# Statistics of a layer norm moved two steps earlier and behind the softmax division, and the root they feed put ahead of the masks on another engine

## The chip, the cores and the metric

The kernel runs on one core of a Trainium2 chip. The metric is the time of one execution on the device in microseconds (us). Two executions of one kernel usually differ by 0.1%, and all that are compared here are in the fast state. The engines are TensorE (PE, matmuls; PEld is its weight load), VectorE (DVE), ScalarE (ACT), GpSimd (POOL) and the queue that issues transfers (SP).

## The reference, cut to what matters

A block over x of shape (2, 256, 128, 128), all in float32: attention over time, attention over the 128 bands (a key counts if it is at most 16 bands away), and a feed-forward part. Each adds to x, and each has its own layer norm.

```python
xt = _ln(x, ...).transpose(0, 2, 1, 3)
x = x + _mha(xt, ..., H_T, causal).transpose(0, 2, 1, 3)
x = x + _mha(_ln(x, ...), ..., H_F, band)      # 16 bands to each side
h = gelu(_ln(x, ...) @ w1.T + b1)
x = x + (h @ w2.T + b2)
```

## The kernel before

Work is cut into groups of 512 tokens. 128 groups of attention over time come first. Then come 16 runs, each of 8 groups of attention over the bands (0 to 7 below) and the feed-forward of the same tokens (8 to 15). One turn of the loop ("step n") works on several groups at once. The order of the calls below is the order of each engine's queue, and in the traces DVE and POOL execute their parts in that order (PE's record has an exception, shown further down).

```python
def statistics(self):                      # DVE
    for i in range(NT): vector.bn_stats(stats[:, i, :], self.src()[:, i, :])
    for i in range(NT): vector.bn_aggr(self.mv[:, i, :], stats[:, i, :])

def root(self):                            # POOL
    gpsimd.tensor_scalar(self.rstd, self.mv[:, :, 1], EPS, None, ALU.add)
    gpsimd.tensor_tensor(self.rstd, self.rstd, path.k.mhalf, ALU.pow)

def normalize(self):                       # DVE, "xh": needs mv and rstd
    for i in range(NT):
        vector.tensor_scalar(self.xh[:, i, :], self.src()[:, i, :],
            self.mv[:, i, 0:1], self.rstd[:, i:i + 1], ALU.subtract, ALU.mult)
# turn: z = block transpose of xh (DVE), four DMAs z -> turned (DRAM)
# fetch: one DMA turned -> xnT, which the group's first matmuls read

# bands: first_mask = 6 affine_selects on POOL (two for each of 3 heads),
#        second_mask = one multiply by the band on DVE (the fourth head)
# divide, bands: t = rp*r0, u = op*r0, oT = (t - 2)*u   (DVE; rp and op in PSUM)
# divide, feed-forward: res = zp + res
# bias: 128x512 sums on POOL, in feed-forward steps only
```

The loop of the kernel before, cut. The groups of matmuls on PE are qp, kp, vp (projections), sp (scores), rp (row sums of the masked exponentials), op (weighted values), yp (output projection), and hp and zp (the two products of the feed-forward part).

```python
for n in range(-11, len(groups) + 2):
    ...
    do(n, "first_half", "first_function", "first_mask")   # sp or hp on PE; exp; masks
    ...
    do_at(n + 1, FeedForward, "fetch")
    do_at(n + 2, FeedForward, "normalize", "turn")
    do_at(n + 3, Attention, "normalize", "turn")
    do_at(n + 3, FeedForward, "statistics", "root")
    do_at(n + 4, OverTime, "root")
    if bands[2]: do(n, "second_mask")
    do(n - 1, "weigh")                                    # rp, op (bands); zp (feed-forward)
    do(n - 1, "invert_exactly" if turn else "invert")
    if bands[2] or turn: do(n - 2, "output", "finish")    # yp
    do(n - 1, "divide")
    if not turn: do(n, "second_half", "second_function")
    if not bands[2]:                                      # biases, the bands' statistics
        do(n, "second_mask", "bias"); do_at(n + A, OverBands, "bias"); ...
    do(n + 1, "queries_keys", ...)                        # qp, kp
    ...
```

## Time and profile before

| | before |
|---|---|
| median of the time | 2792.8 us |
| PE, DVE, ACT, POOL busy | 98%, 82%, 65%, 74% |
| undisturbed band step | 6.436 us |
| undisturbed feed-forward step | 7.006 us |

PE is the bound, and what can be won is its stall. Steps are timed from the first matmul of a group to the first of the next; the prediction says why.

The view below is the timeline of DVE and POOL about steps 5 and 6 of one run. Its columns are start, length, engine, line, operation, out<-in, shapes, count, and in brackets the idle time before it with what ended that.

```profile
1400.45 0.23 POOL L848 TENSOR_SCALAR rstd<-mv 128x4 f32<-128x4 f32 x1
1400.53 0.69 DVE L848 SCALAR_TENSOR_TENSOR oT<-t,u 128x512 f32<-128x512 f32 x1
1400.76 1.36 POOL L848 TENSOR_TENSOR rstd<-rstd,mhalf 128x4 f32<-128x4 f32 x1
1402.15 1.94 DVE L848 TENSOR_SCALAR xh<-x,mv,rstd 128x128 f32<-128x128 f32 x4 [0.94 <-POOL rstd L848]
1402.67 4.27 POOL L848 TENSOR_SCALAR_AFFINE_SELECT pf<-pf 128x512 f32<-128x512 f32 x6 [0.55 <-ACT pf L848]
```

POOL does the root of group 8 after the masks of step 5, so that root ends only at 1402.12. DVE is free at 1401.22 and waits 0.94 us for it. By then the masks of step 6 are about to start, and xh, next to them, takes 1.94 us in place of 1.11.

### The profile page before, as it was taken

What the parts mean: (1) busy time and instruction counts of PE and PEld (TensorE: products, weight loads), DVE (VectorE), ACT (ScalarE), POOL (GpSimd) and SP (SyncE); (2) the same over time, 40 slices, a digit from 0 to 9 for tenths busy, and PEclk for the clock granted to TensorE, in tenths of its full rate; (3) what the DMA queues carried; (4) which work ended last, traced back from release to release, by engine and by line L of the source; (5) the groups of instructions that cost most, each with busy time, mean ns of one, the idle gap of its engine ahead of it and who ended that gap; (6) DMA issues with size and microseconds to landing.
All of it is one profiled execution on the core that took longest, in us unless ns stands there. A gap on an engine that the chain in (4) does not pass through costs nothing.

```text
span 2791.8 us, 103916 instructions
## 1 busy us (share of the span) xinstructions
PE 2733.2 (98%) x42534; PEld 1844.4 (66%) x42534; DVE 2302.8 (82%) x6446; ACT 1800.7 (65%) x3328; POOL 2062.7 (74%) x2569
## 2 busy tenths in 40 slices
PE   4999999999999989999999999999999999999998
PEld 3666666666666656676776766767766667667666
DVE  5888888888888899788787797797887887977975
ACT  2888888788888866646546556456466475564563
POOL 3899999999999996666676676676666766766762
PEclk9999999999999999999999999999999999999999
DMA  5555555545555554543544534535435345444333
GB/s 119 134 148 136 139 139 142 145 131 151 133 142 142 140 137 111 131 123 99 140 102 112 132 104 123 129 96 130 127 100 136 104 108 130 103 125 115 83 99 85
DMA packets 471301, 343.70 MB, mean 123 GB/s; under 512 B 43296, under 2 KB 405152, under 8 KB 470816
## 3 DMA queue, kind: packets, MB, share of 16 engines
q1 hardware_dynamic: 469568, 335.92, 46.5%
q8 instruction: 337, 5.52, 0.8%
q14 instruction: 148, 1.21, 0.1%
q10 hardware_dynamic: 1248, 1.05, 0.1%
HBM read 169.03 MB, written 167.77 MB: 121 GB/s over the span
## 4 chain that ended last, share of the span: by engine, by line
PE 89%; DVE 4%; DMA 3%; POOL 3%; SPq 1%; issue 1%; ACT 0%; DVEq 0%; POOLq 0%
PE zp L848 16%; PE hp L848 15%; PE sp L848 12%; PE op L848 9%; PE qp L848 8%; PE rp L848 7%; PE vp L848 7%; PE kp L848 7%; PE yp L848 7%; DMA xnT<-turned 1%; DVE xh L848 1%; POOL pf L848 1%; DMA turned<-z 1%; POOL rstd L848 1%; POOL pt L848 1%
## 5 line engine op out<-in xcount | busy, mean ns | idle before, releaser
L848 POOL TENSOR_SCALAR_AFFINE_SELECT pf<-pf 128x512 f32<-128x512 f32 x768 | 520.9, 694 | 270.6 <-ACT pf L848 244.3
L848 ACT ACTIVATE hT<-hp,b 128x512 f32<-128x512 f32 x512 | 349.3, 687 | 548.6 <-PE hp L848 539.1
L848 DVE TENSOR_SCALAR xh<-x,mv,rstd 128x128 f32<-128x128 f32 x1536 | 624.0, 467 | 17.4 <-POOL rstd L848 17.4
L848 PEld LDWEIGHTS zp<-w2T_sb,hT 128*128 128x128 f32 x4096 | 476.3, 192 | 56.2 <-issue 54.0
L848 PE MATMUL zp<-w2T_sb,hT 128*128 128x128 f32 x4096 | 479.8, 275 | 0.1
L848 PE MATMUL hp<-xnT,w1f 128*128 128x512 f32 x1024 | 470.5, 596 | 6.7 <-DMA xnT<-turned 5.5
L848 POOL TENSOR_TENSOR rstd<-rstd,mhalf 128x4 f32<-128x4 f32 x384 | 446.9, 1164 | 32.0
L848 ACT ACTIVATE pt<-sp 128x384 f32<-128x384 f32 x1024 | 419.5, 497 | 58.8 <-PE sp L848 58.5
L848 PE MATMUL sp<-qT,kT 32*128 32x128 f32 (+1 forms) x8192 | 397.0, 316 | 0.9 <-ACT kT L848 0.8
L848 POOL TENSOR_SCALAR_AFFINE_SELECT pt<-pt 128x512 f32<-128x512 f32 x512 | 323.0, 652 | 79.6 <-ACT pt L848 79.6
L848 PEld LDWEIGHTS sp<-qT,kT 32*128 32x128 f32 x8192 | 315.3, 185 | 83.1 <-issue 31.4
L848 DVE BATCH_NORM_STATS2 stats<-x 128x6 f32<-128x128 f32 x1536 | 326.5, 273 | 7.7 <-DMA x<-in_x 7.7
L848 POOL TENSOR_SCALAR rstd<-mv 128x4 f32<-128x4 f32 x384 | 88.6, 231 | 298.7 <-DVE mv L848 297.5
L848 ACT ACTIVATE pf<-sp 128x512 f32<-128x512 f32 x512 | 264.3, 603 | 62.4 <-PE sp L848 59.1
L848 PEld LDWEIGHTS hp<-xnT,w1f 128*128 128x128 f32 x1024 | 181.1, 190 | 184.6 <-issue 107.9
L848 PE MATMUL qp<-xnT,wf 128*32 128x512 f32 (+1 forms) x1856 | 270.6, 600 | 26.1 <-DMA xnT<-turned 26.1
L848 PEld LDWEIGHTS yp<-wn,oT 128*32 128x32 f32 (+1 forms) x7808 | 234.1, 111 | 83.8 <-issue 61.8
L848 DVE STREAM_TRANSPOSE z<-xh 128x512 f32<-128x512 f32 x384 | 273.2, 712 | 18.8 <-DMA turned<-z 5.7
L848 PEld LDWEIGHTS vp<-wf,xnT 128*32 128x32 f32 (+1 forms) x7424 | 237.3, 113 | 75.0 <-issue 65.5
L848 PE MATMUL vp<-wf,xnT 128*32 128x128 f32 (+1 forms) x7424 | 271.9, 273 | 0.5 <-DVE t L848 0.5
L848 PE MATMUL yp<-wn,oT 128*32 128x128 f32 (+1 forms) x7808 | 271.1, 273 | 0.3 <-DVE t L848 0.3
L848 DVE TENSOR_TENSOR pf<-pf,band 128x512 f32<-128x512 f32 x128 | 117.4, 917 | 184.8 <-ACT pf L848 177.3
(90 smaller groups left out, 3974.0 us busy)
## 6 DMA issues: line engine op xcount, KB each, us to landing
turned<-z SPq DMA_DIRECT2D x1536, 64.0 KB, 2.1
xnT<-turned SPq DMA_DIRECT2D x384, 256.0 KB, 2.7
x<-in_x SPq DMA_DIRECT2D x128, 256.0 KB, 4.6
x<-res SPq DMA_DIRECT2D x256, 128.0 KB, 3.6
x<-x SPq DMA_DIRECT2D x128, 256.0 KB, 4.1
out<-res SPq DMA_DIRECT2D x256, 128.0 KB, 2.6
w1T_sb<-in_w1T ACTq DMA_DIRECT2D x1, 256.0 KB, 3.7
w2T_sb<-in_w2T ACTq DMA_DIRECT2D x1, 256.0 KB, 4.1
```

The lines of the kernel that those rows point to most:

```text
L848: return self.tc.keep_in_program_order(emit(*args, **kwargs))
```

## The change

Its intent: in band steps DVE should reach the division before it does statistics, and the root should be ready long before normalize needs it.

```diff
             do_at(n + 4, OverTime, "statistics")
             if bands[2] and feeds[1]:
                 self.scalar.preload_act_table_set(EXP_SET)
+            do_at(n + 4, FeedForward, "root")
             do(n, "first_half", "first_function", "first_mask")
@@
             do_at(n + 3, Attention, "normalize", "turn")
-            do_at(n + 3, FeedForward, "statistics", "root")
             do_at(n + 4, OverTime, "root")
@@
             do(n - 1, "divide")
+            do_at(n + 5, FeedForward, "statistics")
             if not turn:
                 do(n, "second_half", "second_function")
```

## The prediction

> **What bounds the kernel now.** I began with the page's busy shares and its list of groups, then read the chain of waits, then the timeline of one run of groups, engine by engine.
>
> ```profile
> PE 2733.2 (98%) x42534; PEld 1844.4 (66%) x42534; DVE 2302.8 (82%) x6446; ACT 1800.7 (65%) x3328; POOL 2062.7 (74%) x2569
> ```
>
> TensorE (PE) is busy for 98% of the span, so nothing that leaves its work alone can win 2%: its whole idle time is 2791.8 - 2733.2 = 58.6 us, and the first groups' load and the tail hold over half of that. Some stall also hides inside "busy", because a group of matmuls is drawn longer when one of them waits. To see it I took, from the trace, the time from the first matmul of each group to the first of the next, and subtracted the shortest such time of that kind.
>
> The change touches only the second half of the kernel (from 1046 us): 16 runs of 8 band-attention groups (0 to 7) followed by 8 feed-forward groups (8 to 15). "Step k" is the turn of the loop whose current group is k. An undisturbed band step costs PE 6.43 us, a feed-forward step 3.44 (hp) + 3.57 (zp) = 7.01 us. The excess over these, summed over the 16 runs, sits in few places:
>
> - Step 7, from scores (sp) to row sums (rp): 0.48 us in every run, 7.7 us in all.
> - Steps 8 and 9, before the first hp matmul: 3.3 us and 1.9 us, in 8 and 5 of the runs, up to 1.0 us each.
> - Step 15, before its first hp matmul: 4.0 us, in 9 runs, 1.7 us in the worst.
> - Step 9 before zp, 0.1 us a run, 1.5 us in all, whose cause I don't see.
>
> Together 18.4 us. That is the prize. The next lines, from timelines of single engines, say what each waits for.
>
> ```profile
> 1404.76 0.83 DVE L848 BATCH_NORM_STATS2 stats<-x 128x6 f32<-128x128 f32 x4
> 1405.51 0.36 DVE L848 BATCH_NORM_AGGREGATE mv<-stats 128x2 f32<-128x6 f32 x4
> 1405.79 0.66 DVE L848 TENSOR_TENSOR pf<-pf,band 128x512 f32<-128x512 f32 x1
> 1406.36 0.68 DVE L848 TENSOR_TENSOR x<-yp,x 128x512 f32<-128x512 f32 x1
> 1406.96 0.68 DVE L848 TENSOR_TENSOR t<-rp,r 128x512 f32<-128x512 f32 x1
> ...
> 1407.70 0.96 PEld L848 LDWEIGHTS sp<-qT,kT 32*128 32x128 f32 x26 [0.19 <-DVE t L848]
> ```
>
> In step 6 VectorE (DVE) does the statistics of a feed-forward group before the division (t, u, oT). Its t ends at 1407.64, and PE's scores of step 7, begun at 1407.20, go on at 1407.70: they need the bank that t reads.
>
> ```profile
> 1737.24 1.06 PE L848 MATMUL yp<-wn,oT 128*32 128x128 f32 x32
> 1739.23 3.67 PE L848 MATMUL hp<-xnT,w1f 128*128 128x512 f32 x8 [0.93 <-DMA xnT<-turned]
> ...
> 2114.26 1.88 PE L848 MATMUL hp<-xnT,w1f 128*128 128x512 f32 x4
> 2117.62 1.96 PE L848 MATMUL hp<-xnT,w1f 128*128 128x512 f32 x4 [1.48 <-DMA xnT<-turned]
> ```
>
> Steps 8 and 15 wait for the transposed input, whose transfers start when normalize and transpose (xh, z) end on DVE. These are late because xh is slow next to POOL:
>
> ```profile
> 2102.18 2.25 DVE L848 TENSOR_SCALAR xh<-x,mv,rstd 128x128 f32<-128x128 f32 x4
> 2105.10 3.11 DVE L848 TENSOR_SCALAR xh<-x,mv,rstd 128x128 f32<-128x128 f32 x4
> ...
> 2105.12 1.27 POOL L848 TENSOR_TENSOR res<-x,rows_sb 128x512 f32<-128x512 f32 x1
> 2106.34 1.27 POOL L848 TENSOR_TENSOR x<-x,orow 128x512 f32<-128x512 f32 x1
> ```
>
> Four xh take 1.11 us when POOL is idle or computes a root, 1.93 beside the masks, 2.95 to 3.1 beside the bias sums. So DVE is busy 6.97 us of the 7.00 from 2086 to 2093: nearly a second bound.
>
> **What the Trainium skill says.** "SBUF — State Buffer", section "Who interferes with whom": DVE and GpSimd share one port pair, whoever issues first keeps it for the instruction; a `tensor_scalar` in a 2-port mode contends, and so does a DVE instruction with two SBUF inputs against a GpSimd one that reads SBUF. The trace agrees: a single xh takes 0.34 us beside a root but 0.72 to 0.78 beside a mask; a mask takes 0.97 instead of 0.63 when DVE multiplies by the band; statistics, one SBUF input, keep 0.27 us whatever POOL does. "PSUM — Partial Sum Buffer", section "Engine vs sequencer instructions", calls the DVE and GpSimd queues strict FIFO: a root placed before the masks holds them back as long as it waits for mv. The trace shows such blocking where POOL sits 1.15 us idle for mv and the bias follows. "Perfetto Trace Analysis", section "GPSIMD Engine Instruction", warns that POOL durations are unreliable and start-to-start spacing is not; I use it below: six masks start to next start take 4.25 us.
>
> **The change part by part.** No instruction is added or removed. Each feed-forward group has 4 BN statistics and 4 aggregates, 1.15 us of DVE (1394.70 to 1395.85), and a root of 0.23 + 1.04 us on POOL, with the start about 0.09 after mv: 1.43 us from mv to the end. Statistics of group m move from step m-3, ahead of the division, to step m-5, behind it; the root goes to step m-4, ahead of the masks. So statistics leave steps 5 to 12 for 3 to 10.
>
> *Steps 3 and 4* gain 1.15 us of DVE. In step 4 DVE idled 1.18 us before its own mask for ACT (1391.30), so statistics at 1388.27 to 1389.42, xh to 1390.5 and z to 1391.2 just fit; step 5 has no normalize. Nothing moves on the path.
>
> *Step 6.* Before, xh(8) began at 1402.15 after 0.94 us of waiting for its root, took 1.94, and the statistics followed. Now its root is two steps old; DVE goes on straight from the statistics of group 10 (1402.3), with POOL in a root: xh ends 1403.4, z 1404.1 (was 1404.83), the band mask about 1405.1, t 1406.3 instead of 1407.64. The scores of step 7 then don't stall: 7.7 us won.
>
> *Steps 8 and 9.* z(8) is 0.77 earlier while PE arrives 0.48 earlier, so each wait shrinks by 0.29: of the eight waits (1.00, 0.53, 0.52, 0.38 and four at or under 0.27) about 1.3 of 3.3 us stays, 2.0 won. In step 7, xh(9) has no masks beside it and no statistics behind it; z(9) ends near 1410.4 instead of 1411.56, 0.67 more than PE's lead: 0.2 of 1.9 us stays, 1.7 won.
>
> *Steps 9 to 15.* A feed-forward step's order on POOL becomes root of the bands' statistics, root of the feed-forward, two biases, all behind statistics at the end of DVE's step, so that xh (right after these) lies beside roots. Groups of four at 1.6, 2.95, 2.95, 2.3 fall to about 1.1. At step 13 the first xh becomes fast, the second still meets biases; z(16) ends near 2107.6 instead of 2108.96. The fetch of group 15 stands behind that of group 16 in the queue, so its 1.5 us wait falls to about 0.2; the smaller ones go: 3.3 of 4.0 us won.
>
> Sum won: 7.7 + 2.0 + 1.7 + 3.3 = 14.7 us.
>
> *The cost: masks.* Before, step 5's masks ran 1396.23 to 1400.48, and PE wanted them at 1401.87, 1.4 us later. Now they wait for statistics and root: division ends 0.46 us after the scores start, statistics end at +1.53, root at +2.96, six masks with 4.25 at +7.21. They now also run under the division's last operation (two SBUF inputs), as under the band multiply: 0.34 more, +7.55, and some 0.08 for the semaphore. PE wants them one step and the scores later, at 6.43 + 1.10 = +7.53. That's a miss of about 0.1 us in steps 4 to 7; a miss at one step delays the next request, so it doesn't add up fully. I take 0.2 us a run, 3.2 us in all.
>
> Net: 14.7 - 3.2 = 11.5 us, 2792.8 to about 2781.3.
>
> **The rivals.** *POOL becomes the bound in steps 4 to 7.* For it: the slack of 1.4 us is spent to the last tenth. If each of four steps missed by 0.3 us, 19 us would be lost and the time be about 2797. Against: a late row sum shifts all that follows, which gives the masks of the next step as much. *DVE was no bound, and other waits take the stalls' place.* PE would start step 8 earlier and meet the transfer of xnT instead: only 5 us won, about 2788. For it: step 8 already waits in half of the runs; against it, z(8) comes earlier by more than PE does. *The relief in the feed-forward part is all there is*, because DVE has slack that PE can't use: 3 us, 2789. *Nothing new happens in masks*: 14.7 us, 2778.
>
> **Range and chances.** The centre is the net sum. The low end, 2775, is all 18.4 us won; the high end, 2790, is the second rival with masks on top. A change of 2% is 56 us: faster by it is beyond PE's stalls, slower by it would take 3.5 us in each of 16 runs, a pile-up of which I see no sign.
>
> **What would show it.** DVE busy falls by about 110 us a kernel: the xh groups lose 7 us a run (two of 0.82, then 0.5, 1.84, 1.84 and 1.2). Four xh of steps 6, 7 and 10 to 12 take 1.1 us. The statistics come right after oT in band steps, and DVE's wait for rstd, 17.4 us in the list of waits, is gone. The scores of step 7 take 1.17 in place of 1.65. Masks of steps 4 to 7 start 1.0 to 1.1 us later, and waits of PE for them appear, 0.1 us each. The prediction is wrong if the row sums stall by more than 0.3 us a step, if xh stays slow, or if hp waits for xnT as much as before.

## The result, and the profile after

The changed kernel took 2786.8 us (2784.58 to 2788.64, 4 runs) against 2792.91 us for the kernel before in the same rounds. The ratio is 0.9977, with a 95% interval of 0.996 to 0.9995. A second submission gave 2784.76 against 2793.06, ratio 0.9971 (0.996 to 0.9982). A ratio is the mean time of one kernel's fast runs over that of the other's in the same rounds, so it is not quite the ratio of the medians. The gain is 6 to 8 us. It lies inside the predicted range, at half to seven tenths of the 11.5 us that were predicted.

The page's first row after:

```profile
PE 2730.3 (98%) x42534; PEld 1867.5 (67%) x42534; DVE 2221.5 (80%) x6446; ACT 1800.0 (65%) x3328; POOL 2079.3 (75%) x2569
```

DVE lost 81 us of busy time: xh fell by 115 (624.0 to 509.2 us in the list of groups), and other operations, oT above all, got slower. PE lost only 3.

The next table gives mean step times over the 16 runs of groups, in the profiled executions. The steps not shown didn't change. "Floor" is the shortest of any run in the kernels here (the fourth row's 8.165 needs a wait just before it; 8.194 is what an undelayed run takes).

| us | floor | before | change | change again |
|---|---|---|---|---|
| scores of step 5 to step 6 | 6.435 | 6.436 | 6.460 | 6.457 |
| scores of step 6 to step 7 | 6.435 | 6.436 | 6.566 | 6.565 |
| scores of step 7 to first hp of step 8 | 3.845 | 4.532 | 4.181 | 4.035 |
| first hp of step 8 to first zp (step 9) | 8.165 | 8.292 | 8.388 | 8.402 |
| zp of step 14 to zp of step 15 (holds the first hp of step 15) | 7.006 | 7.261 | 7.021 | 7.007 |

The sum falls by 0.34 us a run in the first profile, 5.5 us in all (0.49 and 7.8 in the second). A further 1.3 us of that pair's difference in span (2791.8 to 2785.2) lies before the first band scores, where the change does nothing, so it is noise. The gains are at step 7 and step 15. In two rows, and for most runs in the fourth, the change made steps *longer*. The timeline of DVE and POOL in steps 5 and 6 shows how; the run is the one that the lines of before show.

```profile
1394.36 4.58 POOL L848 TENSOR_SCALAR_AFFINE_SELECT pf<-pf 128x512 f32<-128x512 f32 x6
...
1397.37 1.08 DVE L848 SCALAR_TENSOR_TENSOR oT<-t,u 128x512 f32<-128x512 f32 x1
...
1398.37 0.86 DVE L848 BATCH_NORM_STATS2 stats<-x 128x6 f32<-128x128 f32 x4
1399.15 0.36 DVE L848 BATCH_NORM_AGGREGATE mv<-stats 128x2 f32<-128x6 f32 x4
1399.43 1.08 DVE L848 TENSOR_SCALAR xh<-x,mv,rstd 128x128 f32<-128x128 f32 x4
1399.60 0.23 POOL L848 TENSOR_SCALAR rstd<-mv 128x4 f32<-128x4 f32 x1 [0.66 <-DVE mv L848]
1399.91 1.04 POOL L848 TENSOR_TENSOR rstd<-rstd,mhalf 128x4 f32<-128x4 f32 x1
...
1400.92 4.58 POOL L848 TENSOR_SCALAR_AFFINE_SELECT pf<-pf 128x512 f32<-128x512 f32 x6
```

Read it as a ring. The masks start at 1394.36. Their fifth select (affine_select, one of the six instructions of a mask group) ends at 1397.90 (single instructions of the trace). DVE's oT, issued at 1397.37, sits behind it and ends at 1398.45, 1.08 us long instead of 0.69. Statistics follow oT, the root follows them, and the next masks follow the root at 1400.92. The ring takes 6.56 us, and PE's step is 6.44. The Trainium skill's "SBUF — State Buffer", section "Who interferes with whom", says that a DVE instruction with two SBUF inputs contends with a GpSimd one that reads SBUF, for a port that is an exclusive lock. oT has two SBUF inputs, and it ends 0.54 us after the select, which agrees.

What PE sees of it, from its own timeline in the same step, is this:

```profile
1398.85 1.20 PE L848 MATMUL rp<-pf,ones 128*32 128x512 f32 x8
1399.74 1.08 PE L848 MATMUL op<-pf,v 128*32 128x128 f32 x30
1400.61 0.28 PE L848 MATMUL yp<-wn,oT 128*32 128x128 f32 x2
1400.64 0.28 PE L848 MATMUL op<-pf,v 128*32 128x128 f32 x2
...
1404.32 1.17 PE L848 MATMUL sp<-qT,kT 32*128 32x128 f32 x32
```

PE's wait for the masks shows in the first line. The rp group is drawn 1.20 us long, where every rp group of these steps before takes 1.07. In single instructions, the last select ends at 1398.94, and the third head's rp, which reads what that select wrote, starts at 1399.00, 0.14 us behind the first head's (0.01 before). In steps 5 to 7 of all 16 runs it starts 0.05 to 0.06 us after the end of that select, so it is the masks that it waits for. The rp groups of these steps are 0.02, 0.13 and 0.13 us longer than before, which is what the rows above grow by (the last of them shows in the third row's fastest run, 3.972 to a floor of 3.845). The list of waits leaves out gaps so short. Behind it the matmuls get out of order: two of the 32 op matmuls start after the first yp, though op comes first in the program. Each head has its own 32-column strip of the array, and the record fits one head's strip being late while the others go on (inferred; the trace doesn't name the strip). The scores of step 7 take 1.17 us where they took 1.65: the stall that the change was meant for is gone.

### The profile page after: what moved, and what is told of

It is laid out like the page before. It is cut to its first block, busy times and chain, and to the rows that moved or that the text cites. A ratio compares the mean times of both kernels' runs of the same rounds, so it can differ in the third digit from the quotient of the medians.

```text
span 2785.2 us, 103938 instructions
## 1 busy us (share of the span) xinstructions
PE 2730.3 (98%) x42534; PEld 1867.5 (67%) x42534; DVE 2221.5 (80%) x6446; ACT 1800.0 (65%) x3328; POOL 2079.3 (75%) x2569
## 4 chain that ended last, share of the span: by engine, by line
PE 93%; DVE 3%; DMA 2%; POOL 1%; issue 0%; SPq 0%; ACT 0%; DVEq 0%; POOLq 0%
PE zp L848 17%; PE hp L848 16%; PE sp L848 12%; PE op L848 10%; PE qp L848 8%; PE rp L848 8%; PE vp L848 8%; PE yp L848 7%; PE kp L848 7%; POOL pt L848 1%; DMA x<-in_x 1%; DVE xh L848 1%; DMA xnT<-turned 1%; DVE oT L848 0%; POOL rstd L848 0%; DVE stats L848 0%
## 5 line engine op out<-in xcount | busy, mean ns | idle before, releaser
L848 POOL TENSOR_SCALAR_AFFINE_SELECT pf<-pf 128x512 f32<-128x512 f32 x768 | 541.5, 720 | 173.5 <-ACT pf L848 147.1
L848 DVE TENSOR_SCALAR xh<-x,mv,rstd 128x128 f32<-128x128 f32 x1536 | 509.2, 392 | 0.4 <-POOL rstd L848 0.4
L848 POOL TENSOR_TENSOR rstd<-rstd,mhalf 128x4 f32<-128x4 f32 x384 | 441.3, 1149 | 32.0
L848 PE MATMUL sp<-qT,kT 32*128 32x128 f32 (+1 forms) x8192 | 389.5, 315 | 0.8 <-ACT kT L848 0.8
L848 PEld LDWEIGHTS yp<-wn,oT 128*32 128x32 f32 (+1 forms) x7808 | 240.8, 111 | 84.0 <-issue 63.2
L848 PE MATMUL yp<-wn,oT 128*32 128x128 f32 (+1 forms) x7808 | 277.9, 273 | 0.3 <-DVE t L848 0.3
L848 DVE TENSOR_TENSOR res<-zp,res 128x512 f32<-128x512 f32 x128 | 87.6, 685 | 234.8 <-PE zp L848 234.7
```

Source lines behind the costliest of these rows:

```text
L848: return self.tc.keep_in_program_order(emit(*args, **kwargs))
```

## The experiments

Theory A: after the change, masks, the division's last operation, statistics and root form a loop that is longer than PE's step (lock-step), and this eats half of the gain. Theory B: the masks cost nothing, and transfers into step 8 ate it. Theory C: only the feed-forward steps matter. Every kernel gave a correct result. The kernel before had medians of 2792.35 to 2793.06 us beside these runs.

| run | us | ratio to before (95%) |
|---|---|---|
| statistics alone | 2809.34 | 1.0061 (1.0047 to 1.0074) |
| root alone | 3008.8 | 1.0772 (1.0756 to 1.0788) |
| change in band steps alone | 2786.29 | 0.998 (0.9972 to 0.9988) |
| change in feed-forward steps alone | 2802.12 | 1.0032 (1.002 to 1.0044) |
| in the gap | 2776.26 | 0.9939 (0.9926 to 0.9953) |
| shorter root | 2785.68 | 0.9975 (0.9965 to 0.9986) |
| longer root | 2796.56 | 1.0013 (1.0006 to 1.0019) |
| one step earlier, nothing else | 2775.61 | 0.994 (0.9926 to 0.9954) |
| two groups in step 5 | 2783.64 | 0.9965 (0.9951 to 0.9978) |
| the change again | 2784.76 | 0.9971 (0.996 to 0.9982) |

Diffs are against the changed kernel unless they say otherwise.

**Statistics alone.** The statistics stay moved, and the root goes back behind the masks.

```diff
-            do_at(n + 4, FeedForward, "root")              # first
+            do_at(n + 3, FeedForward, "root")              # its old place
```

> The statistics moved as in the change, the root left where it was (step m-3, behind the masks). Theory A (lock-step of masks, division, statistics, root): the masks start at +1.9 us after the scores again, steps 5-6 and 6-7 fall from 6.46 and 6.57 to 6.44 us, the last operation of the division from 1.08 to 0.69 us; but the four xh of steps 6 and 7 lie beside masks again and take 1.9 us, so z(8) ends 4.1 us after the scores of step 6 as before and the first hp of step 8 waits about 0.5 us more a run for its transfer. Net about the changed kernel, 2783 to 2789. Theory B (the gain went to the transfer alone, masks cost nothing): no gain from free masks, later z, 2792 to 2796. Theory C (the gain is in the feed-forward steps, the band steps do not matter): as the changed kernel, 2786, with no shift inside.

This took 2809.34 us, slower than both kernels and outside all three ranges. The mask part came as theory A said: both band rows at 6.436 us. But the step from the first hp to zp took 9.16 us (8.39 with the change), and steps 11 and 12 (each from zp to zp) grew by 0.15 and 0.34. PE waits for transfers there:

```profile
1412.45 3.70 PE L848 MATMUL hp<-xnT,w1f 128*128 128x512 f32 x8
1419.95 1.52 PE L848 MATMUL hp<-xnT,w1f 128*128 128x512 f32 x3 [1.06 <-DMA xnT<-turned]
```

In this kernel nothing holds POOL, so masks, and from step 8 on the biases, begin beside xh: the trace has xh of steps 7 and 8 at 2.1 to 3.0 us, where the change has 1.1. A root that waits at the head of POOL's queue thus does a second thing, which no line of the diff says: it keeps POOL off the shared port while DVE normalizes.

**Root alone.** The statistics go back to their old place, and the root comes first. With the statistics there it can come first only in step m-2, a step later than in the kernel before and two later than in the change. So this run doesn't isolate the root's new place; it tests a late root.

```diff
-            do_at(n + 4, FeedForward, "root")
+            do_at(n + 2, FeedForward, "root")
@@ before the root of OverTime
+            do_at(n + 3, FeedForward, "statistics")
@@ behind the division
-            do_at(n + 5, FeedForward, "statistics")
```

> The other half alone: statistics where they were (group n+3, ahead of the division), the root a step later as POOL's first work (group n+2). Band steps: POOL ends step 5's masks and would do root(8) then as before, so nothing changes there and the 0.48 us stall of step 7 stays. Feed-forward steps: xh of the same step must now wait for a root that stands behind the root of the bands' statistics, 2.5 us later than before, and meets the biases: z late, hp waits for transfers. Slower than before, 2795 to 2830. If the root's place were what won the 6 us, it would be 2787.

3008.8 us: the direction was right, the size far beyond the range. The timeline of DVE in two feed-forward steps:

```profile
1485.45 3.02 DVE L848 TENSOR_SCALAR xh<-x,mv,rstd 128x128 f32<-128x128 f32 x4 [2.80 <-POOL rstd L848]
...
1494.68 3.02 DVE L848 TENSOR_SCALAR xh<-x,mv,rstd 128x128 f32<-128x128 f32 x4 [2.80 <-POOL rstd L848]
```

DVE idles 2.80 us for a root in POOL's queue behind the root of the bands' statistics, and then meets the biases. From one xh to the next it is 9.23 us, where PE's step is 7.01. Steps 12 to 15, from zp to zp, have medians of 12.5, 7.9, 9.4 and 12.4 us. The mean granted TensorE clock was 0.976 in this profile, in place of 0.999.

**The change in band steps alone**, groups 13 to 15 as before.

```diff
-            do_at(n + 4, FeedForward, "root")
+            if bands[2] or turn:
+                do_at(n + 4, FeedForward, "root")
@@
+            if feeds[0]:
+                do_at(n + 3, FeedForward, "statistics", "root")
@@
-            do_at(n + 5, FeedForward, "statistics")
+            if bands[2]:
+                do_at(n + 5, FeedForward, "statistics")
```

> The change in the band steps alone (statistics of groups 8 to 12, roots of 8 to 12); groups 13 to 15 as before. Theory A: the 0.48 us of step 7 are won and some 0.4 us a run are lost to late masks, so near the kernel before: 2790 to 2793, with the steps 5-6, 6-7 at 6.46 and 6.57 us and the hp wait of step 15 (4 us in all) still there. Theory C: 2792 too. Theory B: 2788.

2786.29 us, as good as the whole change, so all three theories missed. The band rows are those of the change (6.454 and 6.566 us), as theory A has it. The row of step 15 is 7.009, so its 4 us of waits went although statistics and roots of groups 13 to 15 stand where they stood before. Theory C falls. In the trace xh(15), the normalize of the group that step 15 waits for, takes 1.08 us here, where the kernel before has 1.7 to 2.8.

**The change in feed-forward steps alone.** To enter them with enough lead, step 8 does the statistics of two groups behind the division and step 9 two roots.

```diff
-            do_at(n + 4, FeedForward, "root")
+            if feeds[1]:
+                if not feeds[0]:
+                    do_at(n + 3, FeedForward, "root")
+                do_at(n + 4, FeedForward, "root")
@@
+            if not feeds[1]:
+                do_at(n + 3, FeedForward, "statistics", "root")
@@
-            do_at(n + 5, FeedForward, "statistics")
+            if turn:
+                do_at(n + 4, FeedForward, "statistics")
+            if feeds[2]:
+                do_at(n + 5, FeedForward, "statistics")
```

> The change in the feed-forward steps alone (groups 12 to 15), band steps as before. Theory A and C: the 3.8 us of step 15 are won and xh of steps 10 to 13 takes 1.1 us, the 0.48 us of step 7 stay: 2788 to 2790. Theory B, by which only what is ahead of step 8 counts: 2792.

2802.12 us, a miss. Step 15 is at its floor, but the first hp of steps 11 and 12 now waits for its transfer: those two steps take 7.39 and 7.44 us. The catching up in step 8, which is my own addition, delays DVE: z of group 11 ends 0.7 us before the reference point (the first zp of step 10) where the change has 2.5. So this run doesn't isolate the feed-forward part. What it shows is that DVE has less than 2 us to spare there.

**In the gap.** Band steps: statistics of group n+4 between z and the band mask, root behind the masks. Feed-forward steps: as in the change.

```diff
-            do_at(n + 4, FeedForward, "root")
+            if feeds[1]:
+                do_at(n + 4, FeedForward, "root")
@@
+            if not feeds[1]:
+                do_at(n + 4, FeedForward, "statistics", "root")
@@
-            do_at(n + 5, FeedForward, "statistics")
+            if feeds[2]:
+                do_at(n + 5, FeedForward, "statistics")
```

> In band steps the statistics stay ahead of the division, in the gap between z and the band mask, but one step earlier than in the kernel before (group n+4), with the root behind the masks; feed-forward steps as in the change. Theory A: no late masks (steps 5-6, 6-7 at 6.44 us, division's last operation 0.69 us), xh fast because it ends before the masks start, z(8) 2.3 us after the scores of step 6, so nearly no wait of hp in step 8, no stall in step 7: 0.65 us a run under the changed kernel, 2775 to 2779. Theory B: the transfer gains 1.2 us too, but masks count for nothing: about 2782. Theory C: 2786.

2776.26 us, as theory A expected and outside the ranges of B and C. All five rows are within 0.03 us of the floor: 6.436, 6.436, 3.846, 8.194, 7.016.

**Shorter root.** DVE adds epsilon behind the statistics, and POOL has the power alone.

```diff
 class FeedForward(Group):
+    def statistics(self):
+        path = self.path
+        super().statistics()
+        self.rstd = path.small.tile([P, NT], F32, name="rstd", bufs=16)
+        path.vector.tensor_scalar(self.rstd, self.mv[:, :, 1], EPS, None, ALU.add)
+    def root(self):
+        path = self.path
+        path.gpsimd.tensor_tensor(self.rstd, self.rstd, path.k.mhalf, ALU.pow)
```

> The changed kernel, with the root's first operation (adding epsilon, 0.23 us on POOL and 0.08 to the next) done on VectorE right behind the feed-forward group's statistics. The loop masks, last operation of the division, statistics, root, masks then takes some 0.2 us less than 6.57 us, so less than PE's 6.44. Lock-step theory: steps 5-6 and 6-7 at 6.44, step 7 to first hp about 0.13 shorter, all four places together 0.3 to 0.4 us a run, 2780 to 2783. Rival (the masks are merely late by a fixed 0.1 us in one step, the rest of the missing gain is transfers): at most 0.1 us a run, 2785 to 2787.

2785.68 us: on the time the rival's range held, not the lock-step's. Inside, the row of step 6 went to 6.437 (from 6.566), as lock-step said, but two things took the gain. The six masks take 4.6 to 4.7 us in place of 4.58, and the ring went only from 6.57 to 6.53, 6.46 and 6.53 us. And the row of step 7 grew to 4.337, since PE comes sooner than the transfer of step 8. The test was weak: the operation that I moved to DVE takes 0.17 us there itself.

**Longer root.** The first operation is done twice, for 0.31 us more.

```diff
 class FeedForward(Group):
+    def longer_root(self):                       # root() with a loop; cut
+        ...
+        for _ in range(2):
+            gpsimd.tensor_scalar(self.rstd, self.mv[:, :, 1], EPS, None, ALU.add)
+        gpsimd.tensor_tensor(self.rstd, self.rstd, path.k.mhalf, ALU.pow)
@@
-            do_at(n + 4, FeedForward, "root")
+            do_at(n + 4, FeedForward, "longer_root")
```

> The changed kernel, with the feed-forward root's first operation done twice: 0.31 us more on POOL ahead of the masks in steps 4 to 7. Lock-step theory: the loop is the bound, so each round takes 0.31 more: steps 5-6 and 6-7 at about 6.76 to 6.88 us, step 4-5 at 6.5 or more, some 1.1 us a run in four places, 2801 to 2806. What the prediction held (a miss at one step delays the next request, so it does not add up): 0.3 us a run once, 2790 to 2793.

2796.56 us, between the two expectations: 10 to 12 us over the change, 0.6 to 0.7 us a run for 0.31 us of root. PE's waits for the masks are now long enough for the list: rp waits for pf of POOL 61 times, 27.4 us in all (two waits, 1.5 us, with the change). The profiled execution is the slowest of the 20 (2802.39 us). The masks' starts, from POOL's timeline, tell why the sum is between:

```profile
1393.47 4.59 POOL L855 TENSOR_SCALAR_AFFINE_SELECT pf<-pf 128x512 f32<-128x512 f32 x6
...
1400.35 4.60 POOL L855 TENSOR_SCALAR_AFFINE_SELECT pf<-pf 128x512 f32<-128x512 f32 x6
1404.92 0.54 POOL L855 TENSOR_SCALAR rstd<-mv 128x4 f32<-128x4 f32 x2
1405.54 1.18 POOL L855 TENSOR_TENSOR rstd<-rstd,mhalf 128x4 f32<-128x4 f32 x1
1406.69 4.59 POOL L855 TENSOR_SCALAR_AFFINE_SELECT pf<-pf 128x512 f32<-128x512 f32 x6
...
1413.62 4.59 POOL L855 TENSOR_SCALAR_AFFINE_SELECT pf<-pf 128x512 f32<-128x512 f32 x6
```

The intervals are 6.88, 6.34 and 6.93 us. The ring takes 6.57 + 0.31 = 6.88, then 6.34, then 6.93 again. In the middle one the masks start late in DVE's step, so that oT falls behind the fourth select (it ends at 1403.20, oT at 1403.75) and not the fifth. The statistics end at 1404.81, before POOL is through with its masks, so the root follows the masks without a wait (no bracket in its line), and POOL's own work, 6.34 us, is all that is left. So the miss does add up over the steps, but not in each.

**One step earlier, nothing else.** Against the kernel *before*, one number:

```diff
-            do_at(n + 3, FeedForward, "statistics", "root")
+            do_at(n + 4, FeedForward, "statistics", "root")
```

> The kernel before with one number changed: statistics and root of group n+4 in place of n+3, in their old places (ahead of the division; behind the masks). Lock-step theory: band steps as in the run that used the gap (6.44 us each, step 7 to first hp 3.85), since those are the same; in the feed-forward steps xh meets the biases again (2.9 us) but one group's statistics fewer are left over, so the wait of step 15 shrinks to about half: 2777 to 2781. If the placing behind the division in the feed-forward steps is needed for the gain of step 15: 2780 to 2782, with 4 us of hp waits there.

2775.61 us, ratio 0.994: 17 us under the kernel before, level with the gap kernel, and a little better than its own range. All rows are again at the floor. The timeline of steps 5 and 6:

```profile
1395.93 0.23 POOL L848 TENSOR_SCALAR rstd<-mv 128x4 f32<-128x4 f32 x1
1396.01 0.69 DVE L848 SCALAR_TENSOR_TENSOR oT<-t,u 128x512 f32<-128x512 f32 x1
1396.24 1.52 POOL L848 TENSOR_TENSOR rstd<-rstd,mhalf 128x4 f32<-128x4 f32 x1
1396.62 1.11 DVE L848 TENSOR_SCALAR xh<-x,mv,rstd 128x128 f32<-128x128 f32 x4
1397.76 0.71 DVE L848 STREAM_TRANSPOSE z<-xh 128x512 f32<-128x512 f32 x1
1398.15 4.25 POOL L848 TENSOR_SCALAR_AFFINE_SELECT pf<-pf 128x512 f32<-128x512 f32 x6 [0.38 <-ACT pf L848]
1398.39 0.83 DVE L848 BATCH_NORM_STATS2 stats<-x 128x6 f32<-128x128 f32 x4
```

The root on POOL is that of the next group, so xh starts the moment oT ends, and ends before the masks begin. The masks wait for ACT again, not for a root. z ends 2.23 us after the scores of step 6 began, against 3.51 in the change and 4.07 before, so no first hp of step 8 waits. In the feed-forward steps xh still takes up to 2.95 us beside the biases, and no step is longer for it.

**Two groups in step 5.** Against the kernel *before*: the same lead from group 9 on, but group 8's root no sooner.

```diff
-            do_at(n + 3, FeedForward, "statistics", "root")
+            if not feeds[4]:
+                do_at(n + 3, FeedForward, "statistics", "root")
+            if at(n + 3, FeedForward):
+                do_at(n + 4, FeedForward, "statistics", "root")
```

> The kernel before, with statistics and root of groups 8 and 9 both in step 5 (where VectorE idles 1.9 us for the band mask's input) and of group n+4 from step 6 on: so each feed-forward step from 8 on has one group less of backlog, as in the run one step earlier, but group 8 has its root no sooner than before. Backlog theory (step 15's wait came from VectorE entering the feed-forward steps a group behind): the wait of step 15 goes, though xh still meets the biases there; xh(8) still waits for its root, so the 0.48 us of step 7 and the waits of step 8 (3.3 us) stay: 2787 to 2790. Collision theory (step 15 waits because xh is slow beside the biases, as the prediction had it): no gain at step 15, 2791 to 2793. If the 17 us of the one-step run don't need the earlier root of group 8: 2776 to 2780.

2783.64 us (2778.62 to 2786.16), in none of the three ranges. Step 15 is at its floor, while the four xh of groups 13 and 14 take 1.6 to 3.0 us, as the backlog theory has it. But the run doesn't refute the collision theory, as it was meant to, because the two normalizes of step 13 have become faster. The lines are of DVE, xh(15) and then xh(16):

```profile
2095.57 1.08 DVE L848 TENSOR_SCALAR xh<-x,mv,rstd 128x128 f32<-128x128 f32 x4
2096.68 0.71 DVE L848 STREAM_TRANSPOSE z<-xh 128x512 f32<-128x512 f32 x1
2097.32 2.83 DVE L848 TENSOR_SCALAR xh<-x,mv,rstd 128x128 f32<-128x128 f32 x4
```

The kernel before has 2.25 and 3.11 us there in the same run (its lines are in the prediction), and 1.7 to 2.8 for xh(15) over all runs. That the stall of step 7 went too was not expected. The second root in step 5 holds the masks of step 6 until xh(8) is done, the same side effect as above. The waits of step 8 stay (2.8 us in all). So what the one-step kernel has over this one is group 8's earlier root.

**The change again**, with no edit.

> The changed kernel once more, for its size in the same call: all theories 2786 to 2787.5, 6 us under the kernel before, with the masks of steps 4 to 7 at 2.9 to 3.2 us after the scores and 0.4 to 0.5 us a run lost there.

2784.76 us, a little under the band expected. The rows are in the result's table; the masks begin 2.9 to 3.2 us after the scores in both profiles.

## Why the prediction was right or wrong

The time, 2786.8 us, is inside the range, and most of the mechanism shows in the trace. The sum came out at about half: 5.5 us in the rows in place of 11.5. That it still lies inside is owed to the range's width, since too much was counted as won and too little as lost.

- *Step 7*: right. The scores take 1.17 us, and no run stalls there: 7.7 us won.
- *Step 8*: mis-sized. I had 2.0 of 3.3 us won. In the first profile nothing was (3.3 us of waits over the fastest such step of that kernel, in 7 runs), so here one of the prediction's own signs of being wrong came true; in the second 2.4 were won. z(8) does end 0.56 us sooner after the scores of step 6 (predicted 0.77). But the time from z to the landed xnT (two transfers and their issue) varies from 5.8 to 8.5 us between runs, and one late transfer (1.6 us) undid the rest. I had treated it as fixed. Shown is the scatter; what makes single transfers late is open.
- *Step 9*: about 0.8 us of waits stay in the first profile, in two runs, where I had 0.2.
- *Steps 9 to 15*: right (3.8 us for 3.3), though narrower than I had it. The fetch of group 15 stands behind z(16). xh(15) begins 8.51 us before zp of step 14 in the kernel before, and again so in all but at most one run of the change, bands alone, one step earlier and two groups. In all four it falls from 1.7 to 2.8 us to 1.08, and xh(16) from 2.9 to 3.1 us to 2.83. So z(16) ends 3.2 us (2.8 in that run) before this zp where it ended 1.2 to 2.5 before it: the 1.4 us that the prediction gave. That groups 13 and 14 become fast too, as I had it, isn't needed: with one step earlier and two groups in step 5 they stay slow. No run holds xh(15) slow and changes nothing else, so this cause rests on the traces' sums.
- *The cost, masks*: this is the step that failed. The prediction said: "a miss at one step delays the next request, so it doesn't add up fully", 3.2 us in all. Measured: 0.02 us at the end of step 5, 0.13 of step 6, 0.13 at step 7 (3.972 for the fastest, to a floor of 3.845), and 0.19 at step 8 in 11 of the 16 runs (8.39 against 8.195), half of that in two more. This comes to (0.02 + 0.13 + 0.13) x 16 + 0.19 x 12 = 6.8 us, and the rp groups, drawn longer by 6.9 us in all, say that PE spent it waiting for the masks (at step 8 too the third rp starts 0.05 to 0.06 us after the last select, in the 13 runs that lose). I had priced the overlap with oT as 0.34 us more for the masks, and forgot that oT itself takes 0.39 us more (0.69 to 1.08) and that the statistics now stand behind it. This closes the ring, and a ring of 6.57 us against a step of 6.44 falls behind by 0.13 each time.

With these sizes: 7.7 + 0 + 1.1 + 3.8 - 6.8 = 5.8 us, near the 5.5 that the rows have. DVE's busy time was to fall by 110 us and fell by 81: xh gave 115, and oT took back about 0.39 x 4 x 16 = 25; the other 9 I didn't trace. One reading was slightly off: six masks take 4.25 us as drawn, but 4.22 from start to the next start.

The two kernels that put statistics into DVE's idle gap, without any wait at the head of POOL's queue, won 16 to 17 of the 18.4 us that the prediction called the prize. (The prize held 1.5 us, at step 9 before zp, that no kernel here changed.) This supports theory A: with free masks, fast xh and an early z, all rows reach the floor. That PE lost the 6.8 us to late masks is shown by its rp groups. That the masks were late by the ring is shown by the starts of the masks in the change and with the longer root, and by the run with the statistics alone, where no root stands before the masks and both band rows are at the floor; the shorter root, a weak test, moved the rows as it says in some steps, not in all.

## What to carry to other kernels

A consumer that waits at the head of a strict queue delays all that stands behind it; if the work behind it can also delay the producer, the two engines form a ring whose length has to be compared with the step of the engine that bounds the kernel. Before moving work behind the critical operation, look for the idle gap ahead of it: the same operation one step earlier, in a gap that was there already, won two to three times as much here with one number changed. And take a part out alone before crediting it: the moved statistics alone made this kernel slower. Then look whether the part could be taken out at all: the root, and the feed-forward steps, could only be tried with something else changed.

## What the Trainium skill lacked or had wrong

- "SBUF — State Buffer", section "Who interferes with whom": the exclusive port is right (oT 0.69 to 1.08 us, xh 1.11 to 1.9 or 3.0 us for four). It lacks that a port wait can close a loop through two queues: 6.57 us against a step of 6.44 here.
- The same section doesn't say that a wait can also help. Here a wait at the head of GpSimd's queue kept it off the port: with it four xh of steps 7 and 8 took 1.1 us, without it up to 3.0, and the kernel went from 2786 to 2809 us.
- "TensorE: Matmul & The Clock Gate", section "The mechanism" (Part 3), says that matmuls are strict FIFO in start and end. The trace has two op matmuls recorded at 1400.64, after yp ones at 1400.61 that follow them in the program: where matmuls run in 32-column strips, a stall can show as disorder and not as a gap.
- No page that I used has the scatter of a route through DRAM (four stores, then a load, with their issue): 5.8 to 8.5 us from the end of z to the landed xnT, for the same bytes at the same step.
